# Storing q and k whole in a graph network's attention, and making their rounded parts during its first chunk

## The chip, the cores and the metric

One core of a Trainium2 chip runs the whole program. The metric is device time in microseconds (us) of one execution. Profiles come from a separate, profiled execution of the same program, whose own time is shown beside its span.

## The reference, cut to what matters

Four layers work on x (3327 x 128) with an adjacency matrix adj (3327 x 3327, ones and zeros). Each layer adds its result to x after a layer norm and a ReLU. The change lies in the second layer, an attention with 128 heads of width 8:

```
h = maximum(layernorm(x), 0)
q = (h @ Wq.T).reshape(128, n, 8)      # n = 3327; k and v alike
a = einsum('dnh,dmh->dnm', q, k) * 128**-0.5
a = softmax(a + adj + adj, axis=2)
out = einsum('dnm,dmh->dnh', a, v).reshape(n, 1024)
x = x + out @ Wo.T
```

The reshape is taken over the flat memory, so that a head is 3327 x 8 consecutive values of the product (row-major), and not a set of columns. The first layer before it is two products with adj; the third and the fourth are a gated update and a second graph product, both after the attention.

## The kernel before

**Projections (L383 to L404).** The nodes run in 26 rows of tiles of 128 nodes (`T = 26`, the last has 127). For each row r PE multiplies the normalised, transposed input `hT` with the weights of q, k and v (two products of 512 columns each). PE's float32 products are exact enough for the reference, but the attention's score product takes operands rounded to a shorter format (F32R). To keep the accuracy, each q and k is stored as two rounded parts: ACT copies the product from PSUM into `s[:, 0]`, rounding it (the high part, L394), DVE subtracts the high part from the product into `s[:, 1]` (the low part, L395), and takes the largest absolute value of the high part (L396). One store per tensor and row then writes both parts to DRAM: `qt` and `kt` have 16 rows (`HL = 2 * E`), rows 0 to 7 the high parts of the 8 components and rows 8 to 15 the low parts, and `GP = 3328 * 128` columns, head after head, 3327 columns each. v goes to `vd` with a column of ones for the softmax's sums. The staging tiles `qk_st` and `v_st` have four buffers each; every store is issued on SP's queue (L379). After the row r = 1 the first group's loads are issued (`load_heads(0, 0)`, L406) and its first keys prepared. This part is ordered by a scheduler, which may bring ready instructions forward.

**Attention (L510 to L549).** The queries run in 7 chunks of 476 columns (`QW`, the last has 471), the heads in 32 groups of 4 (`n_groups`), the keys in 26 steps t of 128 nodes. The loop is chunk, group, step: 7 x 32 = 224 groups, 5824 steps. It stands under `manual_schedule`, so each engine executes the instructions in the order in which the program writes them; SP's queue too. In a step:

- `scores` (L468): PE makes the scores of four heads; each product has 32 rows, the high and low parts of q against those of k. One or two heads are scores with the adjacency added by PE (`late`, tag "I"), the others lie in `early` and get the adjacency added by DVE (L484); one head of the odd steps is instead multiplied by a ready exponential on POOL (L487). ACT takes exponentials: of `late` in every step (L485), and at odd steps of the five heads that DVE prepared in the two steps (L489).
- `weigh` (L491): four steps later PE multiplies the exponentials with v into `acc`; after the last step DVE copies `acc` (L505) and SP stores it (L508). Since weigh is four steps behind, these stores are issued at step 3 of the group that follows.
- at t = 4 `load_heads` (L333) issues the next group's loads on SP: 8 of `k_in`, 16 of `q4`, 4 of `v4`.
- from t = 13 on `key_pair` (L355) copies two tiles of `k_in` per step into F32R with a POOL cast (L360).
- at t = 22 the next chunk's adjacency tiles are loaded, doubled (L260) and stored, about one a group.

`k_in` has one buffer, `q4` and `v4` two each. The general branch (L557 to L631) runs only where a bound on the scores is exceeded, which these inputs don't do; before its work it adds the two parts of q and k together (L558 to L572).

Of the kernel before, what the change touches and what calls it, by code (L numbers as in the profile page):

```python
# [8 lines left out]
F32 = mybir.dt.float32  # L9
# [11 lines left out]
P = 128  # L21
# [32 lines left out]
def kernel(  # L54
# [258 lines left out]

    kt = dpool.tile([HL, GP], F32, name="kt")
    qt = dpool.tile([HL, GP], F32, name="qt")
    vd = dpool.tile([GP, EA], F32, name="vd")
# [9 lines left out]
    def exp_of(a2, c):  # L328
        e = e_pool.tile([P, QW], F32, name="e")
        nc.scalar.activation(e[:, : even(c)], a2[:, : even(c)], AF.Exp)  # L330
        return e

    def load_heads(c, g):  # L333
        q0, _ = q_chunks[c]
        we = even(c)
        k_in = kq.tile([P, NP], F32, name="k_in", bufs=1)
        q4 = kq.tile([P, QW], F32R, name="q4")
        v4 = kq.tile([P, 4, T, EA], F32, name="v4")
        for i in range(4):
            n0 = (4 * g + i) * N  # L340
            for j in range(2):
                r = 32 * i + HL * j
                nc.sync.dma_start(k_in[r : r + HL], kt[:, n0 : n0 + NP])
                for k in range(2):
                    nc.sync.dma_start(
                        q4[r + E * k : r + E * k + E, :we].bitcast(F32),
                        qt[E * j : E * j + E, n0 + q0 : n0 + q0 + we],
                    )
            nc.sync.dma_start(
                v4[:, i].rearrange("p t e -> p (t e)"),  # L350
                vd[n0 : n0 + NP, :].rearrange("(p t) e -> p (t e)", t=T),
            )
        return k_in, q4, v4, []
# [9 lines left out]
    with tc.tile_pool(name="l1", bufs=1) as pool, tc.tile_pool(name="l1_ps", bufs=3, space=PSUM) as ps:  # L363
# [3 lines left out]
        zero = pool.tile([HL, NH], F32, name="zero")  # L367
        nc.vector.memset(zero, 0.0)
        nc.gpsimd.dma_start(vd[N * NH : N * NH + 1, :], zero[:1, :EA])
        for tail in (qt, kt):  # L370
            nc.gpsimd.dma_start(tail[:, N * NH :], zero)

        with tc.tile_pool(name="l1_ln", bufs=1) as ln, tc.tile_pool(name="l1_tp", bufs=2, space=PSUM) as tps:
            hT = transposed(pool, tps, layernorm_relu(ln), "hT")
# [4 lines left out]
                nc.sync.dma_start(dst[r * P + p0 : r * P + p1], src[p0:p1])  # L379


        assert 3 * N + NP <= P * NH
        for r in range(T):  # L383
            kp = rows_of(r)
            lhs = hT[:, r * P : r * P + kp]
            for i, (dst, mx) in enumerate(((qt, q_max), (kt, k_max))):
                pp = ps.tile([P, 2, 512], F32, name="pp", bufs=2)
                for c in range(2):
                    nc.tensor.matmul(pp[:kp, c, :], lhs, w_st[:, i, c * 512 : c * 512 + 512], start=True, stop=True)
                scale = D**-0.5 if i == 0 else 1.0  # L390
                s = st.tile([P, 2, E * NH], F32R, name="qk_st")
                full = pp[:kp].rearrange("p a b -> p (a b)")
                hi = s[:kp, 0].bitcast(F32)
                nc.scalar.activation(s[:kp, 0], full, AF.Copy, scale=scale)  # L394
                nc.vector.scalar_tensor_tensor(s[:kp, 1], full, scale, hi, op0=ALU.mult, op1=ALU.subtract)  # L395
                nc.vector.tensor_reduce(mx[:kp, r : r + 1], hi, AX.X, ALU.max, apply_absolute_value=True)  # L396
                store(dst.rearrange("e (r c) -> r e c", c=NH), s.bitcast(F32).rearrange("p a (e c) -> p (a e) c", c=NH), r, kp)
            pp = ps.tile([P, 2, 512], F32, name="pp", bufs=2)
            for c in range(2):
                nc.tensor.matmul(pp[:kp, c, :], lhs, w_st[:, 2, c * 512 : c * 512 + 512], start=True, stop=True)  # L400
            s = st.tile([P, NH, EA], F32, name="v_st")
            nc.gpsimd.memset(s[:, :, E : E + 1], 1.0)
            nc.scalar.copy(s[:kp, :, :E], pp[:kp].rearrange("p a (c e) -> p (a c) e", e=E))
            store(vd.rearrange("(r c) e -> r (c e)", c=NH), s.rearrange("p c e -> p (c e)"), r, kp)  # L404
            if r == 1:
                first = load_heads(0, 0)  # L406
                while len(first[3]) < T // 2:
                    key_pair(first)
                e_first = [exp_of(a, 0) for a in a_first[1::2]]
# [41 lines left out]
    with tc.tile_pool(name="at_in", bufs=2) as a_pool, tc.tile_pool(name="at_p", bufs=3) as p_pool, tc.tile_pool(  # L451
# [58 lines left out]
        with tc.manual_schedule(engines=engines):  # L510
            groups = [(c, g) for c in range(len(q_chunks)) for g in range(n_groups)]
            steps = [(c, g, t) for c, g in groups for t in range(T)]
            heads = first
            a_t, a_next = a_first, []
            e_t, e_next = e_first, []
            to_store = [(0, t, a2) for t, a2 in enumerate(a_t)]
            begun = {}
            for j, step in enumerate(steps):
                c, g, t = step
                n = c * n_groups + g + 1  # L520
                more = n < len(groups)
                if t == 0 and j:
                    heads = coming
                    if g == 0:
                        a_t, a_next = a_next, []
                        e_t, e_next = e_next, []
                if t % 2 == 0:
                    p8 = p_pool.tile([P, 8, QW], F32, name="p8")
                scores(step, heads, a_t[t], e_t[t // 2], p8)
                begun[j] = (step, heads[2], p8)  # L530
                if j >= ahead:
                    weigh(*begun.pop(j - ahead))
                if t == min(4, T // 2) and more:
                    coming = load_heads(*groups[n])

                if t >= T // 2 and more:
                    key_pair(coming)
                if t == max(T - 4, 0) and c + 1 < len(q_chunks):
                    for _ in range(min(len(to_store), 1 + T // n_groups)):
                        store_adj(*to_store.pop(0))  # L540
                    while len(a_next) < T * (g + 1) // n_groups:
                        to_store.append((c + 1, len(a_next), load_adj(c + 1, len(a_next))))
                        a_next.append(to_store[-1][2])
                if t % 2 and g == n_groups - 1 and c + 1 < len(q_chunks):
                    e_next.append(exp_of(a_next[t], c + 1))
            for j in range(len(steps) - ahead, len(steps)):
                weigh(*begun.pop(j))
            for a in to_store:
                store_adj(*a)  # L549
# [2 lines left out]


    n_once = nc.values_load(n_gen[0:1, 0:1], min_val=0, max_val=1)
    k9 = dpool.tile([EA, GP], F32, name="k9")
    q9 = dpool.tile([EA, GP], F32, name="q9")
    with tc.For_i(0, n_once, 1):  # L557
        with tc.tile_pool(name="ga", bufs=2) as pool:  # L558
            with tc.For_i(0, T, 1) as b:
                for src, dst in ((qt, q9), (kt, k9)):  # L560
                    size = E * GP // T
                    hi = pool.tile([P, size // P], F32, name="hi")
                    lo = pool.tile([P, size // P], F32, name="lo")
                    flat = src.rearrange("e g -> (e g)")
                    nc.sync.dma_start(hi, flat[bass.ds(b * size, size)].rearrange("(p c) -> p c", p=P))
                    nc.sync.dma_start(lo, flat[bass.ds(b * size + E * GP, size)].rearrange("(p c) -> p c", p=P))
                    nc.vector.tensor_add(hi, hi, lo)
                    nc.sync.dma_start(dst.rearrange("e g -> (e g)")[bass.ds(b * size, size)].rearrange("(p c) -> p c", p=P), hi)
            fill = pool.tile([P, NP], F32, name="fill", bufs=1)
            for row, value in ((k9, 1.0), (q9, 0.0)):  # L570
                nc.gpsimd.memset(fill, value)
                nc.gpsimd.dma_start(row[E : E + 1, :].rearrange("o (p g) -> (o p) g", p=P), fill)  # L572
        with tc.tile_pool(name="sh", bufs=2) as pool, tc.tile_pool(name="sh_ps", bufs=2, space=PSUM) as ps:
            with tc.For_i(0, NH, 1) as hd:
                kh = pool.tile([E, N], F32, name="kh")
                qh = pool.tile([E, NP], F32, name="qh")
                nc.sync.dma_start(kh, k9[:E, bass.ds(hd * N, N)])
                nc.sync.dma_start(qh[:, :N], q9[:E, bass.ds(hd * N, N)])
                shift = pool.tile([P, T], F32, name="shift")
                for t in range(T):  # L580
                    kp = rows_of(t)
# [8 lines left out]
                        nc.vector.tensor_reduce(m2[:kp, half : half + 1], a[:kp, h0 : h0 + hw], AX.X, ALU.max)  # L590
                    n_m = len(chunks(N, 2048))
                    nc.vector.tensor_reduce(shift[:kp, t : t + 1], m2[:kp, :n_m], AX.X, ALU.max, negate=True)
                row = q9[E : E + 1, bass.ds(hd * N, NP)].rearrange("o (p t) -> (o p) t", t=T)
                nc.sync.dma_start(row[: P - 1], shift[: P - 1])
                nc.sync.dma_start(row[P - 1 : P, : T - 1], shift[P - 1 : P, : T - 1])
        with tc.tile_pool(name="gb", bufs=2) as pool, tc.tile_pool(name="gb_ps", bufs=2, space=PSUM) as ps, tc.tile_pool(
# [4 lines left out]
            with tc.For_i(0, NH // 4, 1) as g:  # L601
                k4 = pool.tile([P, NP], F32, name="gk4")
                v4 = pool.tile([P, 4, T, EA], F32, name="gv4")
                for i in range(4):
                    nc.sync.dma_start(k4[32 * i : 32 * i + EA, :N], k9[:, bass.ds(g * (4 * N) + i * N, N)])
                    nc.sync.dma_start(
                        v4[:, i].rearrange("p t e -> p (t e)"),
                        vd[bass.ds(g * (4 * N) + i * N, NP), :].rearrange("(p t) e -> p (t e)", t=T),
# [1 line left out]
                for q0, w in chunks(N, QW):  # L610
                    q4 = pool.tile([P, QW], F32, name="gq4")
                    for i in range(4):
                        nc.sync.dma_start(q4[32 * i : 32 * i + EA, :w], q9[:, bass.ds(g * (4 * N) + i * N + q0, w)])
                    for t in range(T):
                        kp = rows_of(t)
                        a = pool.tile([P, QW], F32, name="ga_in")
# [279 lines left out]
```

## Time and profile before

| | us |
|---|---|
| median of 3 runs | 11451.39 (11443.48 to 11453.73) |
| the profiled execution | 11471.65 |
| its span, first to last instruction | 11469.9 |
| granted TensorE clock, mean | 0.985 |
| projections, first store issued to first ACT exponential | 384.9 to 643.1 |
| attention, first ACT exponential to last copy of `acc` | 643.1 to 10565.8 |

| line, engine, what | count | mean ns |
|---|---|---|
| L484 DVE, adjacency added to a head's scores | 14560 | 644 |
| L489 ACT, exponential of five heads | 2912 | 2345 |
| L485 ACT, exponential of one or two heads | 5824 | 923 |
| L487 POOL, product of a head with a ready exponential | 2912 | 1214 |
| L360 POOL, cast of two key tiles | 2912 | 701 |
| L394 ACT, L395 and L396 DVE, q's or k's 1024 columns | 52 each | 1023, 1223, 1208 |

How to read it: a line number is that of the kernel before; busy time is the union of an engine's instructions, which overlap slightly, so that count times mean can be above it. "idle before" names what ended an engine's wait.

### The profile page before, as it was taken

The numbers are of one execution on the slowest core, as the hardware profiler recorded it, in microseconds if no ns is written. First come the engines' busy times: TensorE is split into PE (matmuls) and PEld (weight loads), VectorE is DVE, ScalarE is ACT, GpSimd is POOL, SyncE is SP. The second block draws the span as 40 slices with busy tenths as digits, with TensorE's granted clock in tenths as the row PEclk, the third lists the DMA queues.
The fourth block names the chain that finished last, engine by engine and source line by source line (L and its number), as shares of the span: only waits on it lengthen the run. The fifth ranks groups of instructions, "written<-read, shape, count | busy, mean of one in ns | idle before, by whom it ended". The sixth has DMA issues, their size and how long they took to land. (4 is left out here: it accounts for less than half of the span.)

```text
span 11469.9 us, 212317 instructions
## 1 busy us (share of the span) xinstructions
PE 11060.2 (96%) x80114; PEld 3113.4 (27%) x80114; DVE 9433.5 (82%) x15530; ACT 10214.1 (89%) x9169; POOL 5699.5 (50%) x6205
## 2 busy tenths in 40 slices
PE   9789999999999999999999999999999999999887
PEld 4322222222222222222222222222222222222553
DVE  8578888888888888888888888888888888887464
ACT  0389999999999999999999999999999999998221
POOL 0145555555555555555555555555555555554003
PEclk9899999999999999999999999999999999999998
DMA  7854444343434444444444444434444434343313
GB/s 268 237 118 63 67 64 67 61 69 62 69 61 67 62 69 62 68 62 66 64 66 65 61 67 61 69 60 67 61 68 62 65 57 60 56 61 73 123 57 114
DMA packets 475718, 888.18 MB, mean 77 GB/s; under 512 B 91380, under 2 KB 422629, under 8 KB 439092
## 3 DMA queue, kind: packets, MB, share of 16 engines
q1 hardware_dynamic: 470226, 864.60, 42.6%
q8 instruction: 640, 10.49, 0.4%
q0 software_dynamic: 4448, 9.79, 0.3%
q14 instruction: 404, 3.31, 0.1%
HBM read 763.28 MB, written 110.74 MB: 76 GB/s over the span
## 5 line engine op out<-in xcount | busy, mean ns | idle before, releaser
L484 DVE TENSOR_TENSOR p<-early,a 128x476 f32<-128x476 f32 (+1 forms) x14560 | 8434.5, 644 | 1393.2 <-PE early L479 1160.2
L489 ACT ACTIVATE p<-p 128x2380 f32<-128x2380 f32 (+1 forms) x2912 | 6830.1, 2345 | 8.5
L496 PE MATMUL acc<-p,v 128*9 128x476 f32 (+1 forms) x46592 | 5847.5, 564 | 25.9 <-POOL p L487 7.1
L487 POOL TENSOR_TENSOR p<-p,e 128x476 f32<-128x476 f32 (+1 forms) x2912 | 3535.7, 1214 | 3317.7 <-ACT p L485 3271.5
L485 ACT ACTIVATE p<-late 128x476 f32<-128x476 f32 (+1 forms) x5824 | 4592.2, 923 | 32.3 <-DMA k_in<-kt 21.3
L479 PE MATMUL early<-q,k 32*128 32x476 f32 (+1 forms) x14560 | 2885.5, 477 | 19.9 <-DVE p L484 19.9
L479 PE MATMUL late<-q,k 32*128 32x476 f32 (+1 forms) x8736 | 2797.3, 478 | 64.3 <-ACT p L485 36.2
L360 POOL CAST k<-k_in 128x256 fp32r<-128x256 f32 x2912 | 1943.9, 701 | 1115.9 <-DMA q<-qt 579.2
L479 PEld LDWEIGHTS late<-q,k 32*128 32x128 f32 x8736 | 1065.4, 181 | 4775.4 <-ACT p L485 3318.4
L482 PE MATMUL late<-a,two_i 128*128 128x476 bf16 (+1 forms) x5824 | 2180.8, 374 | 0.0
L479 PEld LDWEIGHTS early<-q,k 32*128 32x128 f32 x14560 | 1147.3, 181 | 26.8 <-DVE p L484 20.6
L496 PEld LDWEIGHTS acc<-p,v 128*9 128x9 f32 x46592 | 709.0, 88 | 1367.8 <-issue 1184.9
L482 PEld LDWEIGHTS <-two_i 128*128 128x128 bf16 x5824 | 556.4, 96 | 1326.6 <-issue 1326.6
L217 PE MATMUL agg_ps<-a,part 128*128 128x512 bf16 (+1 forms) x1638 | 351.7, 375 | 91.7 <-issue 50.1
L177 ACT COPY agg<-agg_ps 128x512 f32<-128x512 f32 x15 | 8.2, 591 | 481.9 <-PE agg_ps L191 290.5
L815 POOL DMA_INDIRECT row<-yd,idx x104 | 99.6, 958 | 461.1 <-DMA yd<-y 393.7
L217 PEld LDWEIGHTS <-part 128*128 128x128 bf16 x1638 | 163.1, 100 | 276.2 <-issue 76.3
L260 POOL TENSOR_SCALAR a<-a_in 128x476 bf16<-128x476 f32 (+2 forms) x156 | 222.5, 1426 | 0.5
L786 ACT ACTIVATE dist<-sp,nsq 128x2048 f32<-128x2048 f32 (+1 forms) x52 | 85.6, 1647 | 114.3 <-PE sp L785 104.0
L394 ACT ACTIVATE qk_st<-pp 128x1024 fp32r<-128x1024 f32 (+1 forms) x52 | 53.2, 1023 | 147.8 <-DMA qt<-qk_st 61.3
L260 POOL TENSOR_SCALAR a<-a 128x476 bf16<-128x476 f32 (+1 forms) x26 | 36.4, 1399 | 295.8 <-DMA a<-in_adjT_dram 295.8
L191 PE MATMUL agg_ps<-a,h 128*128 128x512 f32 (+2 forms) x364 | 148.1, 570 | 24.0 <-DVE h L153 24.0
(186 smaller groups left out, 2602.0 us busy)
## 6 DMA issues: line engine op xcount, KB each, us to landing
k_in<-kt SPq DMA_DIRECT2D x1792, 208.0 KB
v<-vd SPq DMA_DIRECT2D x896, 117.0 KB
a<-in_adjT_dram SPq DMA_DIRECT2D x50, 1663.5 KB
a<-adj SPq DMA_DIRECT2D x78, 831.8 KB
q<-qt SPq DMA_DIRECT2D x3072, 14.9 KB
a_in<-in_adjT_dram SPq DMA_DIRECT2D x125, 238.0 KB
qt<-qk_st SPq DMA_DIRECT2D x25, 1024.0 KB
kt<-qk_st SPq DMA_DIRECT2D x25, 1024.0 KB
```

Of the source, the lines that this page charges most:

```text
L191: nc.tensor.matmul(acc[c][:, :w], lhs[:kp, t, :], a[:kp, c0 : c0 + w], start=(t == 0), stop=(t == T - 1))
L217: nc.tensor.matmul(acc[c][:, :w], part[:, t, :], a[:, c0 : c0 + w], start=(t == 0 and i == 0), stop=(t == T - 1 and i == 2),)
L260: nc.gpsimd.tensor_scalar(a2[:kp, :w], a, 2.0, None, op0=ALU.mult)
L360: nc.gpsimd.tensor_copy(k, slots(k_in)[:, t : t + 2, :])
L479: nc.tensor.matmul(sp[:, :we], pairs[t // 2][r, t % 2, :], q4[r, :we], start=True, stop=ways[i] != "I")
L482: nc.tensor.matmul(late[:, i - n_d, :we], two_i, a2[:, :we], start=False, stop=True)
L484: nc.vector.tensor_tensor(p8[:, places[i], :we], early[i][:, :we], a2[:, :we], op=ALU.add)
L485: nc.scalar.activation(p8[:, places[n_d] : places[3] + 1, :we], late[:, :, :we], AF.Exp)
L487: nc.gpsimd.tensor_tensor(p8[:, places[3], :we], p8[:, places[3], :we], e_a[:, :we], op=ALU.mult)
L489: nc.scalar.activation(p8[:, :5, :we], p8[:, :5, :we], AF.Exp)
L496: nc.tensor.matmul(acc[32 * i : 32 * i + EA, :w], v4[:kp, i, t, :], p8[:kp, PLACES[t % 2][i], :w], start=(t == 0), stop=(t == T - 1),)
L815: nc.gpsimd.indirect_dma_start(out=row, out_offset=None, in_=yd, in_offset=bass.IndirectOffsetOnAxis(ap=idx[:, t, k : k + 1], axis=0),)
```

## The change

q and k are stored whole, in float32, in new DRAM tensors `qf` and `kf`: of the projections' staging tile only one half is left, written by ACT without rounding, and the subtraction L395 is gone. The two rounded parts are made by a new generator, `parting(g)`: for a group of four heads it loads k (then q) as 96 rows of 1109 values (8 components by 12 pieces), POOL copies it piece by piece into F32R (`hi`), DVE subtracts that in place (`lo`), and two stores write both to `kt` (`qt`). Each `yield` ends one action, 20 a group. For groups 0 and 1 all actions are written out after row r = 1 of the projections, ahead of `load_heads(0, 0)`; for groups 2 to 31 one action is taken per step of group g - 2 in chunk 0, after the step's `scores`, `weigh` and, at t = 4, `load_heads`, and ahead of its `key_pair`. `lo` and `hi` have one buffer each.

The loads of `k_in` and `q4` become exactly N and w columns wide, with a POOL memset for the column behind. The general branch reads `kf` and `qf` and no longer adds parts.

```diff
+    kf = dpool.tile([EA, GP], F32, name="kf")
+    qf = dpool.tile([EA, GP], F32, name="qf")
...
+    JW = 12
+    WJ = 4 * N // JW
+    CUT = -(-WJ // 4)
+
+    def parting(g):
+        for src, dst in ((kf, kt), (qf, qt)):
+            lo = kq.tile([E * JW, WJ], F32R, name="lo", bufs=1)
+            hi = kq.tile([E * JW, WJ], F32R, name="hi", bufs=1)
+            full = lo.bitcast(F32)
+
+            def rows(ap, r):
+                return dram(ap, r * GP + 4 * g * N, [[GP, E], [WJ, JW], [1, WJ]])
+
+            nc.sync.dma_start(full, rows(src, 0))
+            yield
+            for c0, w in chunks(WJ, CUT):
+                p = slice(c0, c0 + w)
+                nc.gpsimd.tensor_copy(hi[:, p], full[:, p])
+                yield
+                nc.vector.tensor_sub(lo[:, p], full[:, p], hi[:, p].bitcast(F32))
+                yield
+            nc.sync.dma_start(rows(dst, 0), hi.bitcast(F32))
+            nc.sync.dma_start(rows(dst, E), full)
+            yield
...
     def load_heads(c, g):
+        nc.gpsimd.memset(k_in[:, N:], 0.0)
+        if w % 2:
+            nc.gpsimd.memset(q4[:, w : w + 1].bitcast(F32), 0.0)
...
-                nc.sync.dma_start(k_in[r : r + HL], kt[:, n0 : n0 + NP])
+                nc.sync.dma_start(k_in[r : r + HL, :N], kt[:, n0 : n0 + N])
...
-                        q4[r + E * k : r + E * k + E, :we].bitcast(F32),
-                        qt[E * j : E * j + E, n0 + q0 : n0 + q0 + we],
+                        q4[r + E * k : r + E * k + E, :w].bitcast(F32),
+                        qt[E * j : E * j + E, n0 + q0 : n0 + q0 + w],
...
-                s = st.tile([P, 2, E * NH], F32R, name="qk_st")
-                full = pp[:kp].rearrange("p a b -> p (a b)")
-                hi = s[:kp, 0].bitcast(F32)
-                nc.scalar.activation(s[:kp, 0], full, AF.Copy, scale=scale)
-                nc.vector.scalar_tensor_tensor(s[:kp, 1], full, scale, hi, op0=ALU.mult, op1=ALU.subtract)
-                nc.vector.tensor_reduce(mx[:kp, r : r + 1], hi, AX.X, ALU.max, apply_absolute_value=True)
-                store(dst.rearrange("e (r c) -> r e c", c=NH), s.bitcast(F32).rearrange("p a (e c) -> p (a e) c", c=NH), r, kp)
+                s = st.tile([P, E * NH], F32, name="qk_st")
+                nc.scalar.activation(s[:kp], pp[:kp].rearrange("p a b -> p (a b)"), AF.Copy, scale=D**-0.5 if i == 0 else 1.0)
+                nc.vector.tensor_reduce(mx[:kp, r : r + 1], s[:kp], AX.X, ALU.max, apply_absolute_value=True)
+                store(dst[:E].rearrange("e (r c) -> r e c", c=NH), s.rearrange("p (e c) -> p e c", c=NH), r, kp)
...
             if r == 1:
+                for g in range(2):
+                    for _ in parting(g):
+                        pass
                 first = load_heads(0, 0)
...
                 if t == min(4, T // 2) and more:
                     coming = load_heads(*groups[n])
+                if c == 0 and t == 0 and g + 2 < n_groups:
+                    parts_to_do = parting(g + 2)
+                if c == 0 and g + 2 < n_groups:
+                    for _ in range(-(-20 // T)):
+                        next(parts_to_do, None)
 
                 if t >= T // 2 and more:
                     key_pair(coming)
```

## The prediction

> **What bounds the kernel now.** I read the busy times first, then the stretches, then the timelines of the four engines and of SP's queue.
>
> ```profile
> PE 11060.2 (96%) x80114; PEld 3113.4 (27%) x80114; DVE 9433.5 (82%) x15530; ACT 10214.1 (89%) x9169; POOL 5699.5 (50%) x6205
> ```
>
> The whole-span shares hide two stages of different kind. The windows (columns: stretch, length, busy time and count of PE, PEld, DVE, ACT, POOL, then granted clock, DMA share, GB/s) tell them apart:
>
> ```profile
> 504.47:558.58 54.11, 37.12 (x72) 13.28 (x72) 28.26 (x25) 18.10 (x19) 1.97 (x6) 0.94 1.03 299
> 739.04:783.05 44.01, 43.84 (x342) 10.96 (x342) 38.18 (x68) 44.01 (x40) 25.06 (x27) 1.00 0.47 66
> ```
>
> The first is six rows of tiles of the projections (about 384 to 643 us): the DMA engines are full (1.03), no compute engine is above 70%. A row takes 54.11/6 = 9.02 us, and SP's queue shows it as one long push:
>
> ```profile
> 508.76 1.20 SPq L379 DMA_DIRECT2D qt<-qk_st  x1
> 510.05 4.10 SPq L379 DMA_DIRECT2D kt<-qk_st  x1
> 514.25 3.55 SPq L379 DMA_DIRECT2D vd<-v_st  x1
> ```
>
> The second is one whole group of the attention's chunk 0: ACT is busy for all 44.01 us, DMA is half idle. With 224 groups from 643 to 10566 us, attention is the kernel. Inside the group, SP (four stores of the group before, then the 28 loads of the group to come, then the adjacency tile):
>
> ```profile
> 739.71 1.39 SPq L508 DMA_DIRECT2D ot<-o  x4
> 741.20 0.33 SPq L343 DMA_DIRECT2D k_in<-kt  x1
> ...
> 758.57 0.35 SPq L349 DMA_DIRECT2D v<-vd  x1
> 759.17 0.35 SPq L466 DMA_DIRECT2D adj<-a  x1
> ```
>
> The loads begin only when step 3's copy of `acc` frees the stores, and SP needs until 758.92 to issue them. POOL, ACT and DVE at the same time:
>
> ```profile
> 753.03 1.21 POOL L487 TENSOR_TENSOR p<-p,e 128x476 f32<-128x476 f32 x1 [2.17 <-ACT p L485]
> 756.42 1.21 POOL L487 TENSOR_TENSOR p<-p,e 128x476 f32<-128x476 f32 x1 [2.18 <-ACT p L485]
> 762.69 1.33 POOL L360 CAST k<-k_in 128x256 fp32r<-128x256 f32 x2 [5.06 <-DMA q<-qt]
> ```
> ```profile
> 754.72 1.62 ACT L485 ACTIVATE p<-late 128x476 f32<-128x476 f32 x2
> 756.01 2.41 ACT L489 ACTIVATE p<-p 128x2380 f32<-128x2380 f32 x1
> 758.08 1.65 ACT L485 ACTIVATE p<-late 128x476 f32<-128x476 f32 x2
> 759.37 2.43 ACT L489 ACTIVATE p<-p 128x2380 f32<-128x2380 f32 x1
> ```
> ```profile
> 752.80 2.89 DVE L484 TENSOR_TENSOR p<-early,a 128x476 f32<-128x476 f32 x5 [0.39 <-PE early L479]
> 756.19 2.89 DVE L484 TENSOR_TENSOR p<-early,a 128x476 f32<-128x476 f32 x5 [0.49 <-PE early L479]
> ```
>
> Two steps take 3.37 us. The copy of `acc` at 739.04 closes step 3, so the DVE run at 752.80 is steps 12 and 13 (five adds, 0.578 us apart), L489 at 756.01 is step 13's, and the L487 at 753.03 and 756.42 are steps 11 and 13. DVE ends step 13's adds at 755.69, ACT takes them at 756.01: 0.3 us of slack. POOL may wait 5.06 us for the key loads at step 13 and nobody stops, since weigh comes four steps later.
>
> **The change, part by part.**
>
> *Projections.* Per row, the stores of q and k fall from 1024 to 512 KB each; with v's 576 KB a row falls from 2624 to 1600 KB. At 299 GB/s that is 5.5 us instead of 9.0. PE becomes nearly equal: its twelve passes take 1.98 us per four, 5.9 us a row at the most. The removed DVE subtraction (L395, 1.22 us) was not the bound. 24 rows x (9.0 - 5.9) = 74 us, and about 7 us in the first two rows and 7 in the drain of stores after the last matmul (625.95 to 643). Against it: the parts of groups 0 and 1 are made here, 4 loads and 8 stores of 426 KB (96 rows x 4436 B), 5.1 MB, 17 us at 299 GB/s, and four serial chains of load, copy, subtract, store, in which SP's stores of later rows may stand behind a store that waits for DVE: 0 to 40 us, I take 16. Sum: -55 us, bounds -88 and -20. If it appears, attention starts near 588 us instead of 643.
>
> *Small edits.* One POOL memset of a column per group (at most the 0.33 us of the 128x128 memset) sits in POOL's 2.17 us idle time before L487; without that cover it would be 224 x 0.33 = 74 us of POOL, not of the path. Loads cut to N or w elements, the tail zeros, and the general branch that does not run: 0.
>
> *The parts of groups 2 to 31, in groups 0 to 29 of chunk 0.* One action of `parting` per step: k's load at step 0, copies on POOL at 1, 3, 5, 7, subtractions on DVE at 2, 4, 6, 8, both stores at 9; q's load at 10, copies at 11 to 17, subtractions at 12 to 18, stores at 19. Every engine runs this in program order. So per group 2 loads and 4 stores (2.55 MB) join SP's queue, 8 copies POOL, 8 subtractions DVE.
>
> k's half is early enough: its load stands behind only the last group's tail, where SP is idle for over 20 us (760.6 to 783.7). q's half is not. SP reaches step 9's stores only after the 28 loads, at 759.2, though their data were ready near 748. `lo` and `hi` have one buffer, so q's load waits on SP until both stores have landed, and step 11's copy on POOL waits for that load; step 12's subtraction, the next thing on DVE after 754.5, waits for the copy. Behind it stand step 13's adds, and so L489 of step 13, and ACT has nothing else: the stall is the kernel's.
>
> Its size: fixed latency and rate come from rows that bound them. Latency: the last key load was issued at 758.57 and released POOL at 762.69, 4.1 us of which 1.0 is 117 KB at 119 GB/s, so 3.1; the first ot load after attention (issued 10578.75, DVE L658 released 10584.39, 2.8 to 3.6 us a tile after it) leaves 2.0. Rate: 299 GB/s (the projections' stores) or 119 (740 to 760 us, the loads of k_in, q and v). Two stores, 852 KB: 2.85 or 7.2 us; one load, 426 KB: 1.42 or 3.6. The copy is 278 columns, 0.698 x 278/256 = 0.76 us by L360; the subtraction 3.62 x 278/3327 = 0.30 us by L279, 0.36 with the 0.06 us of DVE's shortest instruction.
> - fast: 759.5 + 2.0 + 2.85 + 2.0 + 1.42 + 1.12 = 768.9; 14.1 us after 754.5, less the slack of 0.3
> - slow: 759.5 + 3.1 + 7.2 + 3.1 + 3.6 + 1.12 = 777.6; 22.8 us
>
> The stores are like the first row in their many partitions, the DRAM side (8 rows) like the second: I take the middle, 18.5 us.
>
> The Trainium skill, page "DMA: Bandwidth & Descriptors", section "Why a DMA increments its semaphore by 16 and not by 1", says that a transfer is spread over the largest number of engines up to 16 that divides the slowest dimension of both sides. By it the new transfers, 8 rows by 96 partitions, would use 8 engines; no row of this trace shows a spread over engines. At half of 299 GB/s that estimate makes the stall 14.1 + 4.3 = 18.4 us with the short latency, against 14.1 if all 16 serve.
>
> After the stall PE restarts at a lower clock: after the idle 20 us before 643 the windows show
>
> ```profile
> 649.00:653.00 4.00, 4.00 (x21) 0.79 (x23) 2.17 (x4) 3.09 (x3) 1.20 (x1) 0.50 0.78 138
> 657.00:661.00 4.00, 4.00 (x34) 0.81 (x26) 3.62 (x7) 3.85 (x4) 1.21 (x1) 1.00 0.46 76
> ```
>
> and L489 came at 649.44, 653.95, 658.04, 661.43: 4.51 and 4.09 us apart instead of 3.37, 1.9 us lost (bounds 0 and 4). So 18.5 + 1.9 = 20.4 us in each of 29 groups = 592. Group 0 differs: its loads are issued before attention begins (638.65 to 656.9), so its two stores go out once step 8's subtraction is done, near 660 on the old clock, q's load is there between 660 + 9.4 = 669 and 678, and DVE needs it near 665: 4 to 13 us, I take 7.
>
> The other subtractions: L487 ends at 757.6, the copy at 758.4, the adds of step 14 at 757.9, so DVE waits 0.5 us and works 0.3: 0.8 us against a slack of 0.3. As PE's next scores do not wait for L489, every second pair absorbs it: 4 x 0.5 = 2 us per group, 60 us in 30 groups (bounds 0, if jitter absorbs all, and 8 x 0.8 x 30 = 190).
>
> Sum: -55 + 592 + 7 + 60 = **+604 us**. The profiled execution took 11471.65 us (span 11469.9, 1.75 around it): it becomes 12076. The median shown is 20 us lower, 11451.4: **12055 us**.
>
> **The rivals.**
> 1. *Both halves stall.* q's stores at step 19, the adjacency transfers and k's next load must be done by step 1 of the next group, 15 us later; by the slow row they need 3.1 + 7.2 + 3.1 + 3.6 = 17 us and 3 us more for 357 KB of adjacency. Some 5 to 11 us more per group: 29 x 8 = 232, 12287 us. For it: the 119 GB/s; against it: SP and DMA are idle there (DMA share 0.12 from 760 to 784).
> 2. *Faster.* q's load lands before DVE needs it, and the subtractions fit into DVE's 0.49 us waits: -55 alone, 11396 us. It would need the stores to be issued by about 745 instead of 759; for it speaks only that DMA is half idle over the group; against it, SP's order.
> 3. *No long stall, but the slots cost.* As 2, with +60 and a few us per group: 11456 to 11600 us.
>
> **How the numbers follow.** Forecast 0.72 (its own range: 29 x 14.1 - 88 = +321 to 29 x 26.8 + 10 + 110 - 20 = +877, that is 11770 to 12330), rival 1 0.09, rival 2 0.12, rival 3 0.07. The range goes from 11600 to 12400: it leaves out rival 2, much of 3 and the ends. 0.2% of this kernel is 23 us, about what can be told from no change. Faster 0.12; same 0.03 (the low end of rival 3); slower 0.85.
>
> **What would show it.** Right: attention starts 50 us earlier; in each group of chunk 0, POOL idle some 15 to 20 us after step 11's L487, released by the load of `lo`, DVE idle as long, ACT's share in chunk 0 near 0.65, groups of 66 us instead of 44; from chunk 1 on 44 us as before. Wrong: the step-9 stores issued ahead of, or among, the 28 loads; the load of q released by something earlier than both stores; groups of chunk 0 under 50 us.

## The result and the profile after

The changed kernel takes 12099 us (median of 4 runs, 12087 to 12116) against 11449 for the kernel before (4 runs): a ratio of 1.057, with an interval of 1.0553 to 1.0587. The forecast was +604 us; +650 was measured. The profiled execution took 12093.0 us, its span 12091.3. The busy times and three rows of the slices over the span (each digit is the busy share of a fortieth, in tenths) show where it lies:

```profile
PE 11151.1 (92%) x80114; PEld 3138.9 (26%) x80114; DVE 9532.5 (79%) x15734; ACT 10257.0 (85%) x9169; POOL 5810.4 (48%) x6717
...
PE   9777767689999999999999999999999999999888
...
ACT  0366666689999999999999999999999999999322
...
PEclk9888888899999999999999999999999999999988
```

Slices 3 to 8 (ACT at 6) are chunk 0, the only chunk in which parts are made. The windows (stretch, length, busy time and count of PE, PEld, DVE, ACT, POOL, then granted clock, DMA share, GB/s) say the same of the 30 groups in which parts are made (591 to 2578 us) and of all the groups behind them:

```profile
591.00:2578.30 1987.30, 1420.44 (x10158) 360.34 (x10158) 1299.82 (x2230) 1348.36 (x1175) 842.56 (x1076) 0.84 0.40 81
2578.30:11229.00 8650.70, 8542.88 (x65547) 2112.94 (x65547) 7391.54 (x12794) 8594.18 (x7639) 4784.11 (x5419) 1.00 0.43 63
```

ACT is busy for 68% of the first and 99% of the second. In the view of the waits (engine and line, whom it waited for: us in all, times, longest) the lost time forms one chain, read from the bottom up:

```profile
ACT p L520 <- DVE p L515: 592.3, 110, 19.9
...
DVE lo L357 <- POOL hi L355: 564.1, 35, 18.8
...
POOL hi L355 <- DMA lo<-qf: 543.1, 31, 18.6
```

One group of chunk 0 shows the links. SP's queue first (start, length, line, transfer):

```profile
982.81 1.39 SPq L539 DMA_DIRECT2D ot<-o  x4
...
1002.31 0.36 SPq L381 DMA_DIRECT2D v<-vd  x1
1002.98 0.67 SPq L359 DMA_DIRECT2D kt<-hi  x1
1004.42 0.64 SPq L360 DMA_DIRECT2D kt<-lo  x1
1010.54 0.71 SPq L351 DMA_DIRECT2D lo<-qf  x1
1028.53 0.64 SPq L359 DMA_DIRECT2D qt<-hi  x1
```

The stores of k's parts leave straight after the last of the 28 loads of the next group; the load of q leaves 6.1 us after the second store, when the single buffer is free. POOL, DVE and ACT of the same group (in brackets the idle time before the instruction, and what ended it):

```profile
1015.39 0.41 POOL L355 CAST hi<-lo 96x278 fp32r<-96x278 f32 x1 [17.86 <-DMA lo<-qf]
```
```profile
1015.83 1.77 DVE L357 TENSOR_TENSOR lo<-lo,hi 96x278 fp32r<-96x278 f32 x1 [17.97 <-POOL hi L355]
1017.53 2.88 DVE L515 TENSOR_TENSOR p<-early,a 128x476 f32<-128x476 f32 x5
```
```profile
1018.76 2.19 ACT L520 ACTIVATE p<-p 128x2380 f32<-128x2380 f32 x1 [19.13 <-DVE p L515]
...
1023.31 2.18 ACT L520 ACTIVATE p<-p 128x2380 f32<-128x2380 f32 x1
...
1027.77 2.19 ACT L520 ACTIVATE p<-p 128x2380 f32<-128x2380 f32 x1 [0.90 <-DVE p L515]
...
1031.24 2.19 ACT L520 ACTIVATE p<-p 128x2380 f32<-128x2380 f32 x1
```

The copy of q's first quarter waits for the load, the subtraction behind it for the copy, and the five adds of the scores behind that; ACT is idle for 19.13 us. Afterwards its long instructions come 4.55, 4.46 and 3.47 us apart instead of 3.37: 2.4 us more. The subtraction at 1015.83 took 1.77 us, where others of the same size take 0.43; the section on the prediction comes back to it.

The account by stages needs care with its partner: in the first trace of before, the stage behind the attention took 904 us, in a second trace of the same kernel (`e7_before_again`, span 11428.2) 860. Against that second trace:

| stage | before, us | after, us | difference |
|---|---|---|---|
| start to the attention's first exponential | 642.8 | 590.4 | -52 |
| to the first copy of `acc` (group 0) | 52.2 | 61.4 | +9 |
| chunk 0, the other 31 groups | 1375.1 | 2020.7 | +646 |
| chunks 1 to 6 | 8498.0 | 8556.1 | +58 |
| behind the attention | 860.1 | 862.6 | +2 |
| span | 11428.2 | 12091.3 | +663 |

### The profile page after: what moved, and what is told of

It is laid out like the page before. It is cut to its first block, busy times and chain, and to the rows that moved or that the text cites. A ratio compares the mean times of both kernels' runs of the same rounds, so it can differ in the third digit from the quotient of the medians.

```text
span 12091.3 us, 213348 instructions
## 1 busy us (share of the span) xinstructions
PE 11151.1 (92%) x80114; PEld 3138.9 (26%) x80114; DVE 9532.5 (79%) x15734; ACT 10257.0 (85%) x9169; POOL 5810.4 (48%) x6717
## 3 DMA queue, kind: packets, MB, share of 16 engines
q14 instruction: 411, 3.37, 0.1%
## 5 line engine op out<-in xcount | busy, mean ns | idle before, releaser
L520 ACT ACTIVATE p<-p 128x2380 f32<-128x2380 f32 (+1 forms) x2912 | 6671.6, 2291 | 611.3 <-DVE p L515 592.3
L527 PE MATMUL acc<-p,v 128*9 128x476 f32 (+1 forms) x46592 | 5921.6, 568 | 62.0 <-POOL p L518 35.2
L516 ACT ACTIVATE p<-late 128x476 f32<-128x476 f32 (+1 forms) x5824 | 4448.3, 867 | 91.8 <-PE late L513 79.7
L510 PE MATMUL early<-q,k 32*128 32x476 f32 (+1 forms) x14560 | 2942.7, 480 | 564.0 <-DVE p L515 562.5
L510 PEld LDWEIGHTS early<-q,k 32*128 32x128 f32 x14560 | 1173.7, 182 | 586.5 <-DVE p L515 582.0
L357 DVE TENSOR_TENSOR lo<-lo,hi 96x278 fp32r<-96x278 f32 (+1 forms) x256 | 173.3, 681 | 565.4 <-POOL hi L355 564.1
L355 POOL CAST hi<-lo 96x278 fp32r<-96x278 f32 (+1 forms) x256 | 107.2, 421 | 567.4 <-DMA lo<-qf 543.1
```

What stands on the lines that cost most here:

```text
L355: nc.gpsimd.tensor_copy(hi[:, p], full[:, p])
L357: nc.vector.tensor_sub(lo[:, p], full[:, p], hi[:, p].bitcast(F32))
L510: nc.tensor.matmul(sp[:, :we], pairs[t // 2][r, t % 2, :], q4[r, :we], start=True, stop=ways[i] != "I")
L516: nc.scalar.activation(p8[:, places[n_d] : places[3] + 1, :we], late[:, :, :we], AF.Exp)
L520: nc.scalar.activation(p8[:, :5, :we], p8[:, :5, :we], AF.Exp)
L527: nc.tensor.matmul(acc[32 * i : 32 * i + EA, :w], v4[:kp, i, t, :], p8[:kp, PLACES[t % 2][i], :w], start=(t == 0), stop=(t == T - 1),)
```

## Experiments

The theory: q's load is late because SP comes to it only behind the 28 loads and two landed stores. The rivals: one buffer instead of two; the bytes; POOL's and DVE's added work. Kernels of one batch share the runs of the kernel before: 11445 us in the first (7 runs), 11436 in the second (13), 11499 in the third (18), so each is compared with its own batch. The unit used below is the group's period in chunk 0, from one copy of `acc` to the next: 44.05 us before (median), 66.08 after. Where `lo` and `hi` have two buffers, the tile `k` of rounded keys has 20 instead of 26, for space.

**Both loads first (`e1_both_loads_first`).** Both loads leave at step 0, into two buffers each; copies, subtractions and stores follow in the same order as in the change.

```diff
-        for src, dst in ((kf, kt), (qf, qt)):
-            lo = kq.tile(..., bufs=1)
-            nc.sync.dma_start(full, rows(src, 0))
-            yield
+        for src, dst in ((kf, kt), (qf, qt)):
+            lo = kq.tile(..., bufs=2)
+            nc.sync.dma_start(jobs[-1][3], rows(src, 0))
+        yield
+        for n, (dst, lo, hi, full) in enumerate(jobs):
```

> Both loads (k and q) are issued at step 0, ahead of the 28 loads of the next group, into two buffers of lo and hi each; copies, subtractions and stores stay at their steps. (The cast key tiles have 20 buffers instead of 26 for the room.) Theory (q's load comes late because SP has it behind the 28 loads and the landing of k's stores): no long stall, groups of chunk 0 at 44 to 45 us, 12099 - 646 = about 11450 us (11420 to 11490). Rival (the extra traffic, or the copies and subtractions themselves, slow the groups): still above 11900 us.

Measured: 11663 us, ratio 1.0194 (1.0177 to 1.0211); groups of 52.85 us. Sixty per cent of the added time per group goes with the load's place and the second buffer (13.2 of 22.0 us; the next kernel puts the buffer at 2.1), which speaks for the theory, but the expectation was missed by 213 us. POOL, then DVE, then ACT in one group:

```profile
1019.06 0.41 POOL L359 CAST hi<-lo 96x278 fp32r<-96x278 f32 x1
1023.64 1.28 POOL L396 CAST k<-k_in 128x256 fp32r<-128x256 f32 x2 [4.17 <-issue]
1024.89 1.19 POOL L522 TENSOR_TENSOR p<-p,e 128x476 f32<-128x476 f32 x1
1026.02 0.41 POOL L359 CAST hi<-lo 96x278 fp32r<-96x278 f32 x1
```
```profile
1026.46 2.98 DVE L361 TENSOR_TENSOR lo<-lo,hi 96x278 fp32r<-96x278 f32 x1 [3.60 <-POOL hi L359]
```
```profile
1030.59 2.19 ACT L524 ACTIVATE p<-p 128x2380 f32<-128x2380 f32 x1 [5.98 <-DVE p L519]
```

The copy at 1026.02 is step 15's. On POOL it stands behind the cast of the keys at step 13, which always waits for the key loads; in another group the same idle time (4.40 us) is put down to the transfer into `k_in`. Before the change that wait was all but covered (at most 0.3 us a group, see below), since the weighting comes four steps later; a DVE subtraction that needs POOL within one step takes the cover away. A second stall stood behind the first. Not all of it is waiting: DVE waits 3.60 us for the copy, and the subtraction then takes 2.98 us instead of 0.43, while POOL's product and key casts run beside it for 2.9 us.

**Two buffers alone (`e2_two_buffers`).** Only `bufs=1` becomes 2 for `lo` and `hi`; q's load stays at step 10.

> Only the number of buffers of lo and hi goes from 1 to 2 (and that of the cast key tiles from 26 to 20), so that q's load need not wait for the landing of k's stores, but stays behind the 28 loads and both stores on SP. Theory: most of the stall is the place behind the 28 loads; POOL gets q at best when the wait of 6.1 us for the stores' landing is gone (11940 us), and if the load shares its engines with the stores only 1.5 to 2 us earlier (12050 us). Rival (the single buffer is the cause): about 11450 us.

Measured: 11987 us, 1.0476 (1.0455 to 1.0497); groups of 63.95 us. SP's queue and POOL:

```profile
1040.57 0.68 SPq L359 DMA_DIRECT2D kt<-hi  x1
1041.81 0.64 SPq L360 DMA_DIRECT2D kt<-lo  x1
1042.50 1.29 SPq L351 DMA_DIRECT2D lo<-qf  x1
```
```profile
1050.89 0.41 POOL L355 CAST hi<-lo 96x278 fp32r<-96x278 f32 x1 [15.17 <-DMA lo<-qf]
```

The load now leaves at once behind the stores, and is there 10.3 us after the first of them instead of 12.4. The buffer is worth 2.1 us a group. What remains is the wait for SP's place behind the 28 loads, and a load that takes 8.4 us from issue where the change's took 4.85, since it now runs beside the two stores.

**The traffic alone (`e3_traffic_alone`).** From group 2 on, the copies and subtractions are left out and both stores write the unsplit values; loads, stores, their order on SP and the single buffer stay.

```diff
-                nc.gpsimd.tensor_copy(hi[:, p], full[:, p])
+                if g < 2:
+                    nc.gpsimd.tensor_copy(hi[:, p], full[:, p])
...
-                nc.vector.tensor_sub(lo[:, p], full[:, p], hi[:, p].bitcast(F32))
+                if g < 2:
+                    nc.vector.tensor_sub(lo[:, p], full[:, p], hi[:, p].bitcast(F32))
...
-            nc.sync.dma_start(rows(dst, 0), hi.bitcast(F32))
+            nc.sync.dma_start(rows(dst, 0), hi.bitcast(F32) if g < 2 else full)
```

> For groups 2 to 31 the copies and subtractions are left out and both stores write the loaded values unsplit, so the parts are wrong; loads, stores, SP's order and the single buffer stay. Theory (the kernel waits on DVE and POOL for q's load, traffic itself is free): about 11430 us (11400 to 11470). Rival (2.55 MB more of transfers per group collide with the loads of the next group): above 11700 us.

Measured: 11608 us, 1.0145 (1.0125 to 1.0166), between the two theories. The groups tell why: those without an adjacency tile take 43.8 to 44.3 us, as before the change, those with one about 51. SP's queue and POOL in one of the latter:

```profile
1023.21 0.71 SPq L351 DMA_DIRECT2D lo<-qf  x1
1027.99 0.64 SPq L361 DMA_DIRECT2D qt<-lo  x1
...
1031.07 1.97 SPq L161 DMA_DIRECT2D a_in<-in_adjT_dram  x1
```
```profile
1036.41 1.40 POOL L260 TENSOR_SCALAR a<-a_in 128x476 bf16<-128x476 f32 x1 [6.76 <-DMA a_in<-in_adjT_dram]
```

The bytes cost nothing. SP's order costs again: q's stores wait for its load, the adjacency tile's load waits behind them, and POOL waits for that tile before it can go on to the weighting. In the change itself this second place is covered, because the long stall has by then let the loads land.

**Twelve rows first (`e4_twelve_rows_first`).** The order of the two outer dimensions in the transfers of the parts is exchanged; the elements and bytes are the same.

```diff
-                return dram(ap, r * GP + 4 * g * N, [[GP, E], [WJ, JW], [1, WJ]])
+                return dram(ap, r * GP + 4 * g * N, [[WJ, JW], [GP, E], [1, WJ]])
```

> The same 96 rows are taken in the order (12 pieces, 8 components) instead of (8, 12), so that the slowest dimension on the DRAM side is 12. If a transfer of this kind uses as many engines as divide both slowest dimensions (the Trainium skill, DMA: Bandwidth & Descriptors), 12 engines instead of 8 take 3.8 instead of 5.7 us for the two stores and 1.9 instead of 2.85 us for the load: 2.85 us less in each of 29 groups, 12015 us. Rival (all 16 engines serve either form, the time is latency): 12100 us.

Measured: 12043 us, 1.0526 (1.0504 to 1.0547); groups of 64.98 us, 1.1 less than the change's, where 2.85 were expected. Two microseconds from the middle of k's two stores, with nothing else moving, first of the change, then of this kernel:

```profile
1006.00:1008.00 2.00, 0.00 (x0) 0.00 (x0) 0.00 (x0) 0.00 (x0) 0.00 (x0) 0.50 0.51 202
```
```profile
1058.00:1060.00 2.00, 0.00 (x0) 0.00 (x0) 0.00 (x0) 0.00 (x0) 0.00 (x0) 0.50 0.74 272
```

A DMA share of 0.51 with 8 rows and 0.74 with 12, and a rate of 202 and 272 GB/s: more engines serve, and in the middle of the transfer the rate rises with them, by 35%. The Trainium skill, page "DMA: Bandwidth & Descriptors", section "Why a DMA increments its semaphore by 16 and not by 1", says that the engines of a transfer are the largest number up to 16 that divides the slowest dimension of both sides: 8 for 8 rows by 96 partitions, 12 for 12 by 96. The two shares agree with it (8/16 and 12/16). The time falls by less, since a transfer doesn't run at that rate from issue to landing: in the mean of 27 groups, q's load is issued 7.9 us after k's first store in the change and 6.5 here, and the copy starts 4.9 and 5.1 us after that. The prediction's estimate took half of 299 GB/s for 8 engines; they reached 202, so that the engines' number alone was worth less than it said.

**Early copies (`e5_early_copies`).** Built on the first, to take POOL's second wait away: both loads at step 0, the eight copies on POOL at steps 1 to 8, ahead of the key casts; each subtraction one step behind its copy, at steps 2 to 9; the stores at 9 and 10; twelve rows first.

```diff
+        last = None
+        for dst, lo, hi, full in jobs:
+            for c0, w in chunks(WJ, CUT):
...
+                if last:
+                    nc.vector.tensor_sub(*last)
                 nc.gpsimd.tensor_copy(hi[:, p], full[:, p])
+                last = (lo[:, p], full[:, p], hi[:, p].bitcast(F32))
```

> Both loads at step 0, the eight copies on POOL at steps 1 to 8, each subtraction one step later, stores at 9 and 10: all of POOL's and DVE's part is done before POOL begins to wait for the next group's keys at step 13. Rows in the order (12, 8), two buffers, 20 cast key buffers. Theory (what was left in e1 is a copy queued on POOL behind the key casts' wait, with DVE waiting for it; transfers cost nothing): groups of chunk 0 at 44.0 to 45.5 us, so 1 us times 30, and 68 us won in the projections as in e1: about 11430 us (11380 to 11480). Rival (four stores in a row hold back the adjacency tile of step 22, as in e3): groups with a tile at 48 to 50 us, 11560 us.

Measured: 11488 us, 1.0038 (1.0024 to 1.0052); groups of 47.3 us, where 44.0 to 45.5 were expected. No long wait is left. Eight subtractions in eight steps overfill DVE: they take 0.73 us each in the mean and not 0.43, as POOL's products run beside every second one; in that stretch ACT waits 0.5 to 0.8 us for the adds, and two steps take 3.6 to 4.7 us instead of 3.37. And chunks 1 to 6, where no parts are made, are each longer than before, as in the changed kernel; the kernels below look into that.

**The projections alone (`e8_projections_alone`).** The parts of groups 2 to 31 aren't made.

```diff
-            n0 = (4 * g + i) * N
+            n0 = (4 * (g % 2) + i) * N
...
-                if c == 0 and t == 0 and g + 2 < n_groups:
-                    parts_to_do = parting(g + 2)
-                if c == 0 and g + 2 < n_groups:
-                    for _ in range(-(-20 // T)):
-                        next(parts_to_do, None)
```

> The parts of groups 2 to 31 are left out; these groups load the parts of group 0 or 1 instead, so the scores are those of other heads. Projections and the parts of the first two groups stay. Theory (the projections give what the prediction's first term says, and the rest of the change is the parts): 53 us less than before, 11396 us, or some 11440 if chunks 1 to 6 are slower for another reason than the parts. Rival (the projections' gain is lost later): 11450 us or above with slower groups in chunk 0.

Measured: 11415 us, 0.9977 (0.9966 to 0.9987), and 1378.7 us for the 31 groups of chunk 0. The projections' gain is there (the attention starts at 590.26 us instead of 643) and less than half of it arrives at the end (20 us): chunks 1 to 6 are 39 us longer in sum than in the second trace of before, in the table below. The measured time lies between the two that the theory allowed.

**Before, again (`e7_before_again`).** The kernel before, unchanged, for a second trace.

> The kernel before, unchanged, for a second trace: does the part behind attention take 904 us again (the changed kernel's takes 863), and 31 groups of a chunk 1373 to 1376 us? If the two are properties of the program: yes to both. If they differ from execution to execution: values between those of the two kernels.

Measured: 11430 us (one run), span 11428.2. It gave the account above, and showed that the chunks repeat within 2.4 us from trace to trace of one kernel. The 31 groups of every chunk, us:

```
chunk                      0       1       2       3       4       5       6
before                1374.4  1373.1  1373.4  1374.6  1375.8  1374.0  1359.7
e7_before_again       1375.1  1374.5  1373.2  1375.2  1375.2  1376.0  1357.4
after                 2020.7  1380.5  1382.3  1380.3  1384.1  1386.1  1376.6
e8_projections_alone  1378.7  1377.1  1379.5  1379.6  1383.6  1380.7  1369.6
e6_old_widths_later   1465.1  1374.4  1378.0  1376.5  1379.7  1381.2  1375.1
e10_spread            1388.3  1377.6  1378.8  1379.2  1380.6  1382.8  1378.3
e9_spread_tensors_..  1387.8  1377.3  1381.3  1380.0  1381.4  1382.8  1377.6
e11_before_tensors_.  1374.1  1374.3  1375.1  1375.9  1379.6  1376.0  1362.7
```

**The old widths (`e6_old_widths_later`).** The early-copies kernel, but from chunk 1 on the keys and q are loaded in the old, even widths, without the added memsets.

```diff
+        kw, w = (NP, even(c)) if c else (N, w)
...
-                nc.sync.dma_start(k_in[r : r + HL, :N], kt[:, n0 : n0 + N])
+                nc.sync.dma_start(k_in[r : r + HL, :kw], kt[:, n0 : n0 + kw])
```

> As e5, but from chunk 1 on k_in and q4 are loaded as wide as in the kernel before (3328 and an even number of columns) and without the memset. Chunks 1 to 6 took some 8 us more each in the changed kernel than before. Theory A (the width of 3327 or the memset is the cause): chunks 1 to 6 back to 1373 to 1376 us for 31 groups, 50 us less than e5. Theory B (something else, such as where tensors lie): as e5.

Measured: 11486 us, 1.0043 (1.003 to 1.0057), chunks 1 to 6 within 2.2 us each of the kernel that it is built on (which has 1375.8, 1378.7, 1378.7, 1378.8, 1381.9 and 1375.7). Widths and memsets aren't the cause.

**Spread out (`e10_spread`).** Both loads at step 0, copies at steps 1 to 8, one subtraction in every second step (4, 6, ... 18), k's stores at 11, q's at 19, twelve rows first.

```diff
+        for step in range(1, 20):
+            if step <= 8:
+                (_, lo, hi, full), p = pieces_[step - 1]
                 nc.gpsimd.tensor_copy(hi[:, p], full[:, p])
+            if step >= 4 and step % 2 == 0:
+                (_, lo, hi, full), p = pieces_[step // 2 - 2]
                 nc.vector.tensor_sub(lo[:, p], full[:, p], hi[:, p].bitcast(F32))
+            if step in (11, 19):
+                dst, lo, hi, full = jobs[step // 19]
```

> Both loads at step 0, copies on POOL at steps 1 to 8 as in e5, but one subtraction only in every second step, 4, 6 .. 18, and the stores at 11 (k) and 19 (q). Theory (no transfer is waited for any more, and DVE's 0.5 us of idle time in two steps holds one subtraction of 0.36 us): groups of chunk 0 at 44.1 to 44.8 us instead of e5's 47.3, 11488 - 30 x 2.8 = about 11405 us, at or below the kernel before. Rival (a subtraction costs ACT its own time wherever it stands): as e5.

Measured: 11457 us against 11499 (6 and 18 runs), 0.9965 (0.9953 to 0.9977); groups of 44.65 us. This order, with `e9_spread_tensors_last` below, beats both kernels, the kernel before by 0.35%. POOL and ACT around the wait for the key loads:

```profile
952.73 1.21 POOL L523 TENSOR_TENSOR p<-p,e 128x476 f32<-128x476 f32 x1 [2.18 <-ACT p L521]
958.87 1.33 POOL L397 CAST k<-k_in 128x256 fp32r<-128x256 f32 x2 [4.93 <-DMA v<-vd]
```
```profile
955.85 2.26 ACT L525 ACTIVATE p<-p 128x2380 f32<-128x2380 f32 x1
957.93 1.49 ACT L521 ACTIVATE p<-late 128x476 f32<-128x476 f32 x2
959.22 2.28 ACT L525 ACTIVATE p<-p 128x2380 f32<-128x2380 f32 x1
```

POOL waits for the keys as it did before the change, 4.93 us, and ACT runs on without a gap, its long instruction every 3.37 us. The parts of a group cost 0.6 us in this order, and 22 in the change's. By the traces of the same batch (the kernel with moved tensors, below, standing for before) the attention starts 71 us earlier (570.9 for 641.6), chunk 0 is 14 us longer and chunks 1 to 6 are 34 us longer: -23 us; the medians of the two are 30 us apart. The start is earlier than the change's 590.4 because the first groups' chains are shorter: two buffers alone brought it to 579.2, twelve rows alone to 584.4.

**The tensors' place in memory (`e9_spread_tensors_last` and `e11_before_tensors_moved`).** In the first, the spread kernel allocates `kf` and `qf` behind all other tensors; in the second, the kernel before gets these two in front, unused.

```diff
-    kf = dpool.tile([EA, GP], F32, name="kf")
-    qf = dpool.tile([EA, GP], F32, name="qf")
     kt = dpool.tile([HL, GP], F32, name="kt")
...
+    kf = dpool.tile([EA, GP], F32, name="kf")
+    qf = dpool.tile([EA, GP], F32, name="qf")
```
```diff
+    kf = dpool.tile([EA, GP], F32, name="kf")
+    qf = dpool.tile([EA, GP], F32, name="qf")
     kt = dpool.tile([HL, GP], F32, name="kt")
```

> As e10, with kf and qf allocated behind the other DRAM tensors, so that kt, qt, vd, ot and the stored adjacency lie where they lay in the kernel before. Theory P (chunks 1 to 6 of the changed kernel and of all its variants take some 4 to 10 us more each because those tensors moved): 31 groups of a chunk back at 1373 to 1376 us, 40 us less than e10. Theory Q (they are slower for another reason): as e10.

> The kernel before, with kf and qf allocated ahead of kt and qt and used for nothing but eight rows of zeros at their ends. Theory P: chunks 1 to 6, and chunk 0 too, at 1378 to 1386 us for 31 groups instead of 1373 to 1376, 11475 us. Theory Q: as the kernel before, 11436 us.

Measured: 11464 us, 0.9972 (0.9961 to 0.9984), and 11487 us, 0.9992 (0.9983 to 1.0001). Chunks 1 to 6 sum to 8280 us in the first (8277 in the spread kernel) and to 8244 in the second (8231 in the trace of before). Most of the effect follows the change and not the place of the tensors in DRAM.

## Why the prediction was right

The step that decided, q's half, went link by link as worked out; the sizes inside it were in part off, in both directions.

- *SP's order.* k's stores leave just behind the 28 loads. From the issue of the first of them to the copy's start the prediction had 8.3 us (fast) to 17.0 (slow) and took the middle, 12.65; 12.4 were measured (1002.98 to 1015.39), 12.8 in the mean of 27 groups. The middle was a choice between two bounds and wasn't worked out, so a hit this close is partly luck. The two-buffer kernel shows that most of it is the place in SP's order, the first kernel that the late load is the greater part of the loss.
- *k's half.* No wait in it, as predicted: POOL was idle for 567.4 us in all before copies of parts, 543.1 of them for `lo<-qf`.
- *Stall and restart.* 18.5 and 1.9 us were forecast, 19.13 and 2.4 measured. One term in the stall was half of its size: the copy and the subtraction behind q's load were priced at 1.12 us (0.76 and 0.36), and took 0.41 and 1.77. In chunk 0 a subtraction takes 0.43 us where POOL does nothing beside it (157 of 231); in step 12 POOL's product and a key cast run beside it for 1.5 us. No step of the prediction had that.
- *The other subtractions.* 2 us a group were forecast, about 0.6 measured in k's half: two pairs of steps take 3.62 and 3.72 us (median of 29 groups) against 3.37 to 3.39. Those of q's half lie in the restart. The estimate let DVE wait for the copy in every second pair; the copy was priced at 0.76 us by a row with another layout and took 0.41. This term was some three times too large, and the stall's a little too small. For the 31 groups the two gave 652 us together, and 646 were measured; that they meet so closely is luck.
- *Group 0.* +9 for +7.
- *Projections.* -52 for -55, but from other parts. A row of stores takes 5.1 us (q's store at 504.77, the next row's at 509.87), not the 5.9 at which PE was to bound it; and SP's queue was held longer than the 16 us taken: between 393 and 460 us no row's store leaves, because of the chains and loads of the first groups. The two errors cancel, by luck.
- *From chunk 1 on.* "44 us as before" failed in the small: 44.6 for 44.3 us a group, and 58 us over six chunks. The sum has no term for this stage, and the effect is larger than the whole miss of 46 us.

The traces tell where these 58 us lie. One pair of steps, the one that ends with the exponentials of step 21, takes 4.00 us in the mean of chunks 1 to 6, against 3.67 in the second trace of before; the other pairs differ by 0.03 us at most. It goes with POOL's wait for the next group's keys at step 13, which is 5.43 us in the mean against 4.96. POOL's idle time before the key casts in the six chunks, in the second trace of before and in the changed kernel (last column but the releasers):

```profile
L360 POOL CAST k<-k_in 128x256 fp32r<-128x256 f32 x2483 | 1656.4, 700 | 946.7 <-DMA v<-vd 413.4 <-DMA q<-qt 392.7 <-DMA k_in<-kt 90.8
```
```profile
L392 POOL CAST k<-k_in 128x256 fp32r<-128x256 f32 x2483 | 1659.4, 703 | 1037.1 <-DMA q<-qt 471.3 <-DMA v<-vd 442.9 <-DMA k_in<-kt 69.2
```

In both traces the pair takes 3.4 us after waits of 4.5 to 4.8 us, 3.8 after 5.1 to 5.5 and 4.2 after 5.5 to 6.0. So the prediction's "nobody stops" while POOL waits 5.06 us was wrong by a little: beyond 4.8 us the wait costs time, 0.3 us a group already in the kernel before, and the changed kernel's keys land 0.5 us later.

What stays open is why they land later. SP ends their issue 0.2 us later (19.61 us after the copy of `acc`, for 19.41), and the rest passes between issue and landing. The lateness remains with the parts not made at all (a wait of 5.30 us), with the old widths (5.23) and with either place in DRAM; the kernel before with the tensors moved has 5.09, and 13 us of the loss. No run moved only the place of tiles in SBUF, which `lo` and `hi` shift. That the key tile with 20 buffers plays no part in it was not tried by itself, though the change and the projections alone, both with 26, have the effect too.

Of the rivals, none came: there was no stall in k's half, and nothing hid the stall of q's. The spread order comes near the faster outcome that the second rival described (0.9965), but by another way than the one it named: the loads leave ahead of the burst, while the rival needed the stores to.

## What to carry to other kernels

In a program whose engines and queues run in written order, a step moved into a loop is priced by what stands ahead of it in each queue that it enters, not by its own length: here 0.4 us instructions and a hidden transfer cost 22 us a group behind 28 loads, and 0.6 us when the loads left before them and the subtractions were spread out. A stall can cover a second one (the keys on POOL, the adjacency tile on SP), so after the first is mended, look again for what is late next before counting the gain. And an engine with slack, as POOL with its idle 4 to 5 us for the keys, keeps that slack only as long as nothing that others need soon is queued behind its wait; an idle time that has so far cost little can already stand at its limit, as this one did.

## What the runs showed of the hardware

- Exchanging two outer dimensions of the same transfer changed the DMA share from 0.51 to 0.74 and the rate in its middle from 202 to 272 GB/s; per busy engine that is 25 and 23 GB/s (202 / (16 x 0.51), 272 / (16 x 0.74)).
- DVE's subtraction of two tiles in SBUF (96x278) took 0.43 us with POOL idle. With POOL's products and key casts beside it, it grew by about the time that they ran: to 1.77 us with 1.5 us of them (28 cases in the changed kernel), to 2.98 with 2.9 (`e1_both_loads_first`). The adds of the scores beside the same casts kept their length (five in 2.88 us, at 1017.53).
- After 19 us without matmuls the granted clock of PE was 0.50. This window is the 8 us from 1.8 us after the restart, at 0.83 in the mean:

```profile
1020.00:1028.00 8.00, 7.97 (x56) 1.84 (x52) 5.92 (x11) 6.06 (x7) 3.86 (x5) 0.83 0.00 0
```

- Two executions of one kernel differed by 44 us behind the attention alone; the 104 indirect gathers there took 166 us from the first to the last in one, and 130 in the other. By the traces it goes with the batch and not with the kernel: that stage takes 904 to 909 us in the first trace of before and in the three of the third batch, and 857 to 863 in the nine others. A stage by stage account needs a trace of the kernel before from the same batch.
